# Column-quarter sums of a gated recurrent layer: squares, gates and dots in one group, and the sums of o's squares taken once in the feed-forward

## The chip, the cores and the metric

The kernel runs on one core of a Trainium2 chip. The metric is the device time of one execution in microseconds (us). Three runs of the kernel before took 1411.43, 1412.17 and 1412.77 us; the median is 1412.17. One more execution was profiled: 1412.02 us, of which the profile's span, from the first to the last instruction, is 1410.2.

The core has five engines that run side by side, each with its own queue of instructions: TensorE (PE in the profile, its weight loads PEld), VectorE (DVE), ScalarE (ACT), GpSimd (POOL) and SyncE (SP). Here SP only issues transfers (DMAs), and POOL issues those that add to what lies at their target.

## The reference

The input x is one sequence of 2048 tokens with 512 channels. After a layer norm (xn) two branches are computed and multiplied:

```
q, k, v = conv4(silu(xn @ W))          # 16 heads of 128, causal depthwise conv of 4 taps
q, k    = rope(q), rope(k), each divided by its norm over the head
out     = sum over lags s = 0..3 of (q . k[t-s]) * D**-0.5 * sigmoid(a[t-s] * b) * v[t-s]
s       = (out * rsqrt(mean(out**2) + eps) * norm_w * silu(xn @ Wz)) @ Wout
g       = silu((relu(xn @ sign(Wup).T * up_scale) @ sign(Wdown).T) * down_scale * out_scale)
result  = x + s * g
```

a and b are xn @ Wa and xn @ Wb, one number a head. Three kinds of sums over a head or over all channels matter here: the squares of q and k (for their norms), the products of q with the lagged k (the dots), and the squares of out over all 2048 channels (for the root mean square).

## The kernel before, in words

Tokens run along the free axis, 512 to a block (TB), in NTB = 4 blocks; channels lie on the 128 partitions. The 16 heads are worked on two at a time, NP = 8 pairs p = 0..7 in a block.

**The attention's steps.** step(p, b) (line 608) is software-pipelined: it computes q, k and the products of pair p for block b+1, and v, the weighted sum and the gated output of pair p for block b. It is called for b = -1 (block 0's q and k alone, beside the feed-forward of the first 512 tokens), for b = 0, 1 and 2, and the last block's v part has a loop of its own (line 829). InOrder (line 68) keeps the order of the program on TensorE (pe), VectorE (dve) and, where it is used, POOL (pool); line 76, which most rows of the profile name, is its call. The other instructions of ACT, SP and POOL are put in order by the planner that builds the program. In a step TensorE makes pq (16 passes), pk, pv, on even p the output projection po of two finished pairs (four chunks c of 8 passes), and pz.

**Column quarters.** The sums over partitions are matmuls with 32 columns of weights; add (line 429) sends the result to one of four strips of 32 partitions of a bank (tile_position). Four matmuls to the four strips run together. An f32 matmul stands in the trace as two passes, so a group of four appears as x8. The kinds are:
- squares: products (line 366) squares q and k into sq0 and sq1 (line 384), a POOL transfer adds the two, and sum_squares (line 434) adds a pair's sums. Two pairs fill the four strips. It is called in products on even p, between pk and pv, and at a change of block before norms.
- dots: sum_dots (line 445), four strips for the four lags. It is called in output_projections (line 596): halfway through po (after two chunks) when one is due, at once otherwise.
- gates: gate_products (line 231) makes a and b, ab in the profile; four stores to ab_dram follow, three of them accumulating, on POOL. It is called for block 0 after step 0, and for block b+2 in step 7 before pv. gate (line 251) reads them back later.
- sums of o (so): sums_of_o (line 454), two strips, once a block, after the block's last output projection. Its input is a tile squares[b] in pool vs: ACT writes the squares of pair 0's o there, and for the others ACT writes them to o2 (in xnT's first block, or for b = 0 in the second half of the weighted sum's tile te2) and a POOL transfer adds them to squares[b]. Two small transfers put the result in ss_dram.

**Pools.** vs holds what the v part needs (weights, v, bc, te, oz, z, wo, part). mm is a pool of six banks of PSUM. att.close() (line 873) gives back vs, mm and the rest, and the feed-forward opens the pools ff (SBUF, on the same side as vs), ph (three banks) and pf (four banks). ff's first transfers are the loads of down (3 x 1 MB, POOL) and of x, y and g (256 KB each, SP).

**The feed-forward.** For b = 1, 2, 3 and hidden chunks f, TensorE makes ph (8 passes in two f32r terms), ACT and VectorE turn it into hid, and two iterations later pf takes it (8 passes over four banks). Two chunks are made ahead, in the attention's last banks (line 866). ends (line 882) loads x, y and g for a block; gate scales y by rms, which comes from ss_dram by one load, a square root on ACT and a reciprocal on VectorE (lines 870 to 872), and multiplies the branches.

Of the kernel before, what the change touches and what calls it, by code (L numbers as in the profile page):

```python
# [54 lines left out]
TB = 512  # L55
# [26 lines left out]
def recurrent_layer(ctx: ExitStack, tc: tile.TileContext, a: dict, out: bass.AP):  # L82
# [29 lines left out]
    ab_dram = dram.tile([LW, HALO + S], F32, name="ab_dram")  # L112
    ss_dram = dram.tile([NTB, TB], F32, name="ss_dram")
    signs_dram = {n: dram.tile([P, NFC, HID], F32R, name=f"{n}_signs") for n in ("up", "down")}
    f_dram = dram.tile([TB, HID], F32, name="f_dram")
# [77 lines left out]

    means = {}
    means = {}
# [170 lines left out]
    def products(p, b, q, between=None, beside_k=None):  # L366
# [16 lines left out]

        sq = [qks.tile([P, 2, TB], F32, tag=f"sq{j}", name=f"sq{j}" + n, bufs=2 - j) for j in range(2)]
        for j in range(2):
# [48 lines left out]
    def sum_squares():  # L434

        if not squares_due:
            return
        if squares_due[0][0] == 0:
            banks["squares"] = sums.tile([P, TB], F32, tag="squares", name="squares")
        for p, sq in squares_due:  # L440
            for i in (1, 0):
                add(banks["squares"], 2 * (p % 2) + 1 - i, of_head[:, p], sq[:, i, :], p < 2, p >= NP - 2)
        squares_due.clear()

# [8 lines left out]

    def sums_of_o(b):

        so = mm.tile([P, TB], F32, tag="mm", name=f"so{b}")
        for j in range(2):
            add(so, j, ones, squares[b][:, j], True, True)
        row = vs.tile([P, HID], F32, tag="part", name=f"so_sb{b}", bufs=4)
        nc.scalar.copy(row[0 : 2 * LW], so[0 : 2 * LW])  # L460
        nc.gpsimd.dma_start(ss_dram[b : b + 1], row[0:1])
        nc.gpsimd.dma_start(ss_dram[b : b + 1], row[LW : LW + 1], accum_op=ALU.add)

    squares = {}
    rows = {}
# [59 lines left out]
    def weighted(p, b, v):  # L525
# [19 lines left out]
        dve.tensor_tensor(o, o, parts[0][:, 1], ALU.add)  # L545

        if p == 0:
            squares[b] = vs.tile([P, 2, TB], F32, tag="ss", name=f"ss{b}", bufs=1)
            nc.scalar.activation(squares[b], o, AF.Square)
        else:  # L550

            o2 = xnT[:, p % 2 * 2 : p % 2 * 2 + 2, HALO : HALO + TB] if b else parts[1][:, 0]
# [55 lines left out]
    def step(p, b, beside_q=None, beside_k=None):  # L608
# [6 lines left out]
        if change and b:  # L615
            sum_squares()
            norms(b)
# [19 lines left out]

        output_projections(sum_dots if due else None)
        if change:
# [65 lines left out]
    with tc.tile_pool(name="pre", bufs=1, side="right") as pre:  # L705
# [64 lines left out]
        for p in range(NP):  # L770
# [9 lines left out]
            if p + 2 < NP:  # L780
                fetch(*groups[p + 2])
            if p == 0:
                gate_products(0)
            elif p == 2:
                gate(0)
# [10 lines left out]
    load(vs, "z", 0, last)  # L796
    sum_squares()
    norms(last)
# [70 lines left out]
    nc.sync.dma_start(out_scale, a["out_scale"].partition_broadcast(P))  # L869
    nc.sync.dma_start(ss_acc, ss_dram.rearrange("b (c p) -> p (b c)", p=P))  # L870
    nc.scalar.activation(rms, ss_acc, AF.Sqrt, bias=eps_rms, scale=1.0 / CH)
    dve.reciprocal(rms, rms)
    att.close()

    with tc.tile_pool(name="ff", bufs=1, side="right") as ff, tc.tile_pool(
        name="ph", bufs=3, space=PSUM
    ) as phs, tc.tile_pool(name="pf", bufs=1, space=PSUM) as pfs:
        down = ff.tile([P, NFC - NFD, HID], F32R, name="down")
        for f in range(NFD, NFC, G):
            nc.gpsimd.dma_start(down[:, f - NFD : f - NFD + G], signs_dram["down"][:, f : f + G])  # L880

        def ends(b, banks=None):
# [54 lines left out]
        for b in range(1, NTB):  # L937
            pf = [pfs.tile([P, HID], F32, name=f"pf{c}") for c in range(TC)]
            for f in range(2, NFC + 2):
# [6 lines left out]
                if b == 1 and f == 2:  # L946
                    scale, gate = ends(0)
                if b == 1 and f in (6, 8, 10, 12):
                    scale(f // 2 - 3)
                    gate(f // 2 - 3)  # L950
                if b > 1 and f < 2 + TC:
# [111 lines left out]
```

## Time and profile before

| | us |
|---|---|
| time, median of three runs | 1412.17 |
| time of the profiled execution | 1412.02 |
| its span | 1410.2 |
| TensorE busy (3970 passes) | 1399.2 (99%) |
| VectorE busy | 1197.2 (85%) |
| ACT busy | 610.3 (43%) |
| POOL busy | 237.3 (17%) |
| squares: 128 passes of 128x32 weights | first 72.0, last 1046.1 |
| dots: 168 passes | first 53.4, last 1054.2 |
| gates (ab): 32 passes | first 31.2, last 738.9 |
| sums of o (so): 16 passes | first 503.8, last 1226.3 |

The page begins with a busy line for each engine. A line of the timeline has the start, the length, the engine, the source line, the operation, the tiles (out<-in), the shapes and the number of instructions merged into it; in brackets stand the idle time of the engine just before it and what ended it, so far as semaphores show it. Passes overlap, so the distance of two starts tells more than the lengths. A line of transfers has the tiles, the queue, the number, the size of each and the median time from issue to landing.

### The profile page before, as it was taken

To read this page: it belongs to the slowest core of one execution; us is meant where nothing else is said; L and a number is where in the kernel's file an instruction comes from. 1 tells how busy PE (TensorE), PEld (TensorE's weight loads), DVE (VectorE), ACT (ScalarE), POOL (GpSimd) and SP (SyncE) were. 2 spreads that over 40 slices of the span, in tenths; PEclk is the share of its full clock that TensorE was granted. 3 is DMA by queue.
4 is the path that set the end of the run, shared out by engine and by line. 5 is a ranking of instruction groups with operands and counts; after the bars stand their busy time and mean duration, and the time that the engine had idled before them with its cause. 6 is when DMAs were issued, how large, how long until landed. Compare 5 with 4: busy or idle time off the path is not lost.

```text
span 1410.2 us, 12492 instructions
## 1 busy us (share of the span) xinstructions
PE 1399.2 (99%) x3970; PEld 687.7 (49%) x3970; DVE 1197.2 (85%) x1243; ACT 610.3 (43%) x1181; POOL 237.3 (17%) x317
## 2 busy tenths in 40 slices
PE   9999999999999999999999999999999999999998
PEld 6555544344444444444444444444444444578886
DVE  7999999999999999999999899999994998146454
ACT  7566555445444544454434534444442333232122
POOL 2222121111212121112122212121211121200000
PEclk9999999999999999999999999999999999999999
DMA  9989577988988689978985799787848998672020
GB/s 316 284 226 198 126 200 170 238 217 173 199 215 194 141 181 237 227 175 191 224 187 143 163 233 216 178 193 177 165 93 199 226 257 186 123 246 89 24 90 30
DMA packets 104465, 259.21 MB, mean 184 GB/s; under 512 B 18832, under 2 KB 19344, under 8 KB 100048
## 3 DMA queue, kind: packets, MB, share of 16 engines
q0 software_dynamic: 35776, 104.89, 38.3%
q1 hardware_dynamic: 68624, 153.53, 37.5%
q8 instruction: 32, 0.52, 0.1%
q14 instruction: 33, 0.27, 0.1%
HBM read 157.67 MB, written 35.68 MB: 137 GB/s over the span
## 4 chain that ended last, share of the span: by engine, by line
PE 58%; DVE 28%; DMA 5%; issue 4%; ACT 3%; SPq 1%; POOL 0%; DVEq 0%; ACTq 0%; POOLq 0%
PE pq L76 9%; DVE q L76 8%; PE pk L76 8%; PE ph L76 8%; PE pf L76 8%; PE pz L76 8%; PE po L76 8%; DVE te L76 7%; PE pv L76 6%; DVE v L76 4%; DVE k L76 4%; DVE pr L76 3%; DMA bc<-co_dram 2%; DMA co_dram<-rk 1%; PE dots L76 1%
## 5 line engine op out<-in xcount | busy, mean ns | idle before, releaser
L76 PE MATMUL po<-wo,oz 128*128 128x512 f32 x512 | 225.9, 595 | 1.6 <-DVE oz L76 1.6
L76 PE MATMUL pq<-xnT,wq 128*128 128x512 f32 (+1 forms) x528 | 226.5, 581 | 0.2 <-ACT xnT L76 0.2
L76 PE MATMUL pv<-xnT,wv 128*128 128x512 f32 x512 | 226.4, 594 | 0.0
L76 PE MATMUL pz<-xnT,wz 128*128 128x512 f32 x512 | 225.3, 592 | 0.5 <-ACT rv L313 0.5
L76 PE MATMUL pk<-xnT,wk 128*128 128x512 f32 x512 | 225.2, 592 | 0.0
L76 DVE SCALAR_TENSOR_TENSOR k<-rk,conv_w,k 128x512 f32<-128x512 f32 x192 | 142.1, 751 | 24.1 <-ACT k L325 19.5
L76 DVE TENSOR_TENSOR te<-v,bc 128x2048 f32<-128x2048 f32 x64 | 143.9, 2288 | 19.4 <-DMA bc<-co_dram 18.1
L76 PEld LDWEIGHTS pq<-xnT,wq 128*128 128x128 f32 x528 | 98.7, 189 | 124.5 <-issue 113.4
L76 PEld LDWEIGHTS po<-wo,oz 128*128 128x128 f32 x512 | 96.1, 190 | 128.6 <-issue 110.0
L76 PEld LDWEIGHTS pv<-xnT,wv 128*128 128x128 f32 x512 | 95.7, 189 | 127.7 <-issue 116.9
L76 DVE SCALAR_TENSOR_TENSOR q<-rq,conv_w,q 128x512 f32<-128x512 f32 x192 | 141.5, 749 | 19.3 <-ACT q L325 14.8
L76 PEld LDWEIGHTS pz<-xnT,wz 128*128 128x128 f32 x512 | 96.5, 189 | 124.6 <-issue 118.7
L76 PEld LDWEIGHTS pk<-xnT,wk 128*128 128x128 f32 x512 | 96.6, 189 | 120.5 <-issue 116.9
L76 DVE SCALAR_TENSOR_TENSOR v<-rv,conv_w,v 128x512 f32<-128x512 f32 x192 | 141.3, 750 | 6.9 <-ACT v L325 2.4
L76 DVE SCALAR_TENSOR_TENSOR q<-q,turns 128x1024 f32<-128x1024 f32 (+1 forms) x128 | 127.1, 1014 | 2.3
L76 DVE TENSOR_TENSOR pr<-q,k 128x2048 f32<-128x2048 f32 x52 | 117.3, 2286 | 0.9
L700 ACT ACTIVATE hid<-ph,up_scale 128x512 f32<-128x512 f32 x64 | 44.0, 687 | 120.5 <-PE ph L76 118.5
L76 DVE CAST hid_hi<-hid 128x512 fp32r<-128x512 f32 x64 | 27.2, 425 | 71.8 <-ACT hid L700 71.8
L76 PE MATMUL ph<-xs_hi,up 128*128 128x512 f32 x192 | 76.4, 398 | 0.7 <-ACT so_sb L460 0.7
L76 PE MATMUL ph<-xs_lo,up 128*128 128x512 f32 x192 | 75.8, 395 | 0.0
L76 DVE TENSOR_TENSOR te<-te,te 128x2048 f32<-128x2048 f32 x32 | 73.3, 2292 | 1.1
L594 POOL DMA_DIRECT2D s_dram<-part x48 | 50.7, 1231 | 70.1 <-ACT part L588 66.5
(147 smaller groups left out, 1655.4 us busy)
## 6 DMA issues: line engine op xcount, KB each, us to landing
bc<-co_dram SPq DMA_DIRECT2D x128, 256.0 KB, 7.3
pr<-pr POOLq DMA_DIRECT2D x72, 256.0 KB, 6.4
wq<-in_wq_dram SPq DMA_DIRECT2D x32, 512.0 KB, 6.6
wk<-in_wk_dram SPq DMA_DIRECT2D x32, 512.0 KB, 6.6
sq<-sq POOLq DMA_DIRECT2D x32, 512.0 KB, 6.5
wv<-in_wv_dram SPq DMA_DIRECT2D x32, 512.0 KB, 8.0
wz<-in_wz_dram SPq DMA_DIRECT2D x32, 512.0 KB, 5.7
wo<-in_wo_dram SPq DMA_DIRECT2D x32, 512.0 KB, 6.3
```

The source lines that it names most:

```text
L76: return self.tc.keep_in_program_order(getattr(self.engine, op)(*args, **kwargs))
L594: nc.gpsimd.dma_start(rows, part, accum_op=ALU.add)
L700: nc.scalar.activation(hid, ph, AF.Relu, scale=up_scale[:, f : f + 1])
```

## The change

The sums of squares and the gates move to where the dots are. A function strips in step runs halfway through the output projection on even p (or wherever dots are due): the squares of the pairs p-2 and p-1, on p = 6 the gates of block b+2 (on p = 1 of b = -1 those of block 0), and the dots that are due. sum_squares takes the pair at which it stops. sq0 has three buffers instead of two. gate(0) comes after step 3 instead of step 2.

The squares of o are no longer summed in SBUF. All pairs write o2, and POOL's transfers go to o2_dram, pair 0's plainly and the others accumulating. The four blocks' squares are loaded (512 KB each, SP) as the first tile of ff, ss; sums_of_o runs once, in the first feed-forward block at f = 4, between ph and pf, with four strips for the four blocks, and its copy goes to ss_dram by four small transfers on SP. The root and the reciprocal come at f = 8 instead of at the end of the attention, and the first block's scale and gate at f = 8, 10, 12, 14 instead of 6, 8, 10, 12.

```diff
+    o2_dram = [dram.tile([P, 2, TB], F32, name=f"o2_dram{b}") for b in range(NTB)]
...
-        if p % 2 == 0:
-            sum_squares()
+        if p == 0:
+            sum_squares(p)
...
-        sq = [... bufs=2 - j) for j in range(2)]
+        sq = [... bufs=3 - 2 * j) for j in range(2)]
...
+    def sum_squares(last):
+        while squares_due and squares_due[0][0] != last:
+            p, sq = squares_due.pop(0)
+            if p == 0:
+                banks["squares"] = sums.tile([P, TB], F32, tag="squares", name="squares")
             for i in (1, 0):
                 add(banks["squares"], 2 * (p % 2) + 1 - i, of_head[:, p], sq[:, i, :], p < 2, p >= NP - 2)
...
+        o2 = xnT[:, p % 2 * 2 : p % 2 * 2 + 2, HALO : HALO + TB] if b else parts[1][:, 0]
+        nc.scalar.activation(o2, o, AF.Square)
         if p == 0:
-            squares[b] = vs.tile([P, 2, TB], F32, tag="ss", name=f"ss{b}", bufs=1)
-            nc.scalar.activation(squares[b], o, AF.Square)
+            pool.dma_start(o2_dram[b], o2)
         else:
-            o2 = xnT[...] if b else parts[1][:, 0]
-            nc.scalar.activation(o2, o, AF.Square)
-            pool.dma_start(squares[b], o2, accum_op=ALU.add)
+            pool.dma_start(o2_dram[b], o2, accum_op=ALU.add)
...
-        if p == NP - 1:
-            outputs_due.append(lambda midway: sums_of_o(b))
...
-        if p == NP - 1 and b + 2 < NTB:
-            gate_products(b + 2)
...
-        output_projections(sum_dots if due else None)
+        def strips():
+            if p and p % 2 == 0:
+                sum_squares(p)
+            if p == NP - 2 and b + 2 < NTB:
+                gate_products(b + 2)
+            if p == 1 and not at:
+                gate_products(0)
+            if due:
+                sum_dots()
+        output_projections(strips if p % 2 == 0 or due else None)
...
-    nc.sync.dma_start(ss_acc, ss_dram.rearrange("b (c p) -> p (b c)", p=P))
-    nc.scalar.activation(rms, ss_acc, AF.Sqrt, bias=eps_rms, scale=1.0 / CH)
-    dve.reciprocal(rms, rms)
     att.close()
...
+        ss = ff.tile([P, NTB, 2, TB], F32, name="ss")
+        for b in range(NTB):
+            nc.sync.dma_start(ss[:, b], o2_dram[b])
         down = ff.tile([P, NFC - NFD, HID], F32R, name="down")
...
+        def sums_of_o():
+            so = phs.tile([P, TB], F32, name="ph")
+            for j in range(2):
+                for b in range(NTB):
+                    add(so, b, ones, ss[:, b, j], j == 0, j == 1)
+            row = ff.tile([P, TB], F32, name="row")
+            nc.scalar.copy(row, so)
+            for b in range(NTB):
+                nc.sync.dma_start(ss_dram[b : b + 1], row[LW * b : LW * b + 1])
+            nc.sync.dma_start(ss_acc, ss_dram.rearrange("b (c p) -> p (b c)", p=P))
...
+                if b == 1 and f == 4:
+                    sums_of_o()
+                if b == 1 and f == 8:
+                    roots()
+                if b == 1 and f in (8, 10, 12, 14):
+                    scale(f // 2 - 4)
+                    gate(f // 2 - 4)
```

More of the change, by code (lines that the diff above doesn't have):

```diff
@@ L192, in first_layer_norm @@
         return lambda: (transpose(2), transpose(3))
-    means = {}
     means = {}
@@ L382, in products @@
             beside_k()
-        sq = [qks.tile([P, 2, TB], F32, tag=f"sq{j}", name=f"sq{j}" + n, bufs=2 - j) for j in range(2)]
+        sq = [qks.tile([P, 2, TB], F32, tag=f"sq{j}", name=f"sq{j}" + n, bufs=3 - 2 * j) for j in range(2)]
         for j in range(2):
@@ L432, in add @@
         pe.matmul(rows, heads, src, start=start, stop=stop, tile_position=(0, LW * s))
[L434 to L440, printed above, removed]
+    def sum_squares(last):
[3 more added lines that the diff above has]
+                banks["squares"] = sums.tile([P, TB], F32, tag="squares", name="squares")
             for i in (1, 0):
                 add(banks["squares"], 2 * (p % 2) + 1 - i, of_head[:, p], sq[:, i, :], p < 2, p >= NP - 2)
-        squares_due.clear()
     def sum_dots():
@@ L452, in sum_dots @@
                 add(banks["dots"], s, heads, pr[:, s, :], p == 0, last and pr is prs[-1])
[L454 to L464, printed above, removed]
     rows = {}
@@ L545, in weighted @@
         dve.tensor_tensor(o, o, parts[0][:, 1], ALU.add)
+        o2 = xnT[:, p % 2 * 2 : p % 2 * 2 + 2, HALO : HALO + TB] if b else parts[1][:, 0]
+        nc.scalar.activation(o2, o, AF.Square)
         if p == 0:
-            squares[b] = vs.tile([P, 2, TB], F32, tag="ss", name=f"ss{b}", bufs=1)
-            nc.scalar.activation(squares[b], o, AF.Square)
-        else:
-            o2 = xnT[:, p % 2 * 2 : p % 2 * 2 + 2, HALO : HALO + TB] if b else parts[1][:, 0]
-            nc.scalar.activation(o2, o, AF.Square)
-            pool.dma_start(squares[b], o2, accum_op=ALU.add)
+            pool.dma_start(o2_dram[b], o2)
+        else:
+            pool.dma_start(o2_dram[b], o2, accum_op=ALU.add)
         return o
@@ L615, in step @@
         if change and b:
-            sum_squares()
+            sum_squares(p)
             norms(b)
@@ L636, in step @@
             v = values(p, b, raw)
-        output_projections(sum_dots if due else None)
+        def strips():
+            if p and p % 2 == 0:
+                sum_squares(p)
+            if p == NP - 2 and b + 2 < NTB:
[5 more added lines that the diff above has]
+        output_projections(strips if p % 2 == 0 or due else None)
         if change:
@@ L781, in recurrent_layer @@
                 fetch(*groups[p + 2])
-            if p == 0:
-                gate_products(0)
-            elif p == 2:
+            if p == 3:
                 gate(0)
@@ L796, in recurrent_layer @@
     load(vs, "z", 0, last)
-    sum_squares()
+    sum_squares(None)
     norms(last)
@@ L880, in recurrent_layer, with roots @@
             nc.gpsimd.dma_start(down[:, f - NFD : f - NFD + G], signs_dram["down"][:, f : f + G])
+        def sums_of_o():
[8 more added lines that the diff above has]
+            nc.sync.dma_start(ss_acc, ss_dram.rearrange("b (c p) -> p (b c)", p=P))
+        def roots():
+            nc.scalar.activation(rms, ss_acc, AF.Sqrt, bias=eps_rms, scale=1.0 / CH)
+            dve.reciprocal(rms, rms)
         def ends(b, banks=None):
@@ L947, in recurrent_layer @@
                     scale, gate = ends(0)
-                if b == 1 and f in (6, 8, 10, 12):
-                    scale(f // 2 - 3)
-                    gate(f // 2 - 3)
+                if b == 1 and f == 4:
[5 more added lines that the diff above has]
+                    gate(f // 2 - 4)
                 if b > 1 and f < 2 + TC:
```

## The prediction

> **What bounds the kernel now.** I read the page's busy line first, then TensorE's timeline at the places the change touches, then the queues at the start of the feed-forward.
>
> Busy line of the page, and TensorE's timeline at 0, 207 to 355 and 1098 us:
>
> ```profile
> PE 1399.2 (99%) x3970; PEld 687.7 (49%) x3970; DVE 1197.2 (85%) x1243; ACT 610.3 (43%) x1181; POOL 237.3 (17%) x317
> ...
> 1.59 4.63 PE L76 MATMUL unread<-still 128*128 128x512 f32 x6 [1.59 <-DVE still L665]
> ...
> 207.42 7.14 PE L76 MATMUL pv<-xnT,wv 128*128 128x512 f32 x16
> 214.49 1.92 PE L76 MATMUL dots<-pr,of_head 128*32 128x512 f32 x16
> 216.34 7.14 PE L76 MATMUL pq<-xnT,wq 128*128 128x512 f32 x16
> 223.31 7.03 PE L76 MATMUL pk<-xnT,wk 128*128 128x512 f32 x16
> ...
> 264.62 1.07 PE L76 MATMUL squares<-sq,of_head 128*32 128x512 f32 x8
> ...
> 272.59 1.88 PE L76 MATMUL po<-wo,oz 128*128 128x512 f32 x4
> 276.02 5.42 PE L76 MATMUL po<-wo,oz 128*128 128x512 f32 x12 [1.55 <-DVE oz L76]
> ...
> 330.54 7.03 PE L76 MATMUL pk<-xnT,wk 128*128 128x512 f32 x16
> 337.51 1.06 PE L76 MATMUL squares<-sq,of_head 128*32 128x512 f32 x8
> 338.50 7.14 PE L76 MATMUL pv<-xnT,wv 128*128 128x512 f32 x16
> 345.47 7.03 PE L76 MATMUL po<-wo,oz 128*128 128x512 f32 x16
> ...
> 1098.30 7.14 PE L76 MATMUL pz<-xnT,wz 128*128 128x512 f32 x16 [0.54 <-ACT rv L313]
> ```
>
> TensorE sets the time: 99% busy, and a run of 16 full passes takes 6.87 us wherever it stands, 0.43 a pass. It waits in three places only: 1.7 us at 274 (for oz), 0.7 at 1097, 0.7 at 1227 (below). Elsewhere a us off TensorE is a us off the kernel, as long as nothing is late.
>
> TensorE, POOL and SP where the feed-forward begins, then transfers issued at 1227 and at 1234 to 1236, and the engines' table for 1237 to 1246 and for the end (its last columns are granted clock, DMA share and GB/s):
>
> ```profile
> 1226.31 1.05 PE L76 MATMUL so<-ss,ones 128*32 128x512 f32 x4
> 1228.08 0.51 PE L76 MATMUL ph<-xs_hi,up 128*128 128x512 f32 x1 [0.72 <-ACT so_sb L460]
> ...
> 1231.53 0.76 POOL L462 DMA_DIRECT2D ss_dram<-so_sb  x1 [2.67 <-DMA ss_dram<-so_sb]
> 1234.50 1.69 POOL L880 DMA_DIRECT2D down<-down_signs  x3 [2.21 <-PE ph L76]
> ...
> 1234.60 0.71 SPq L889 DMA_DIRECT2D x<-in_x_dram  x1
> ...
> s_dram<-part POOLq DMA_DIRECT2D x1, 256.0 KB, 3.7
> ...
> down<-down_signs POOLq DMA_DIRECT2D x3, 1024.0 KB, 8.4
> x<-in_x_dram SPq DMA_DIRECT2D x1, 256.0 KB, 6.9
> y<-s_dram SPq DMA_DIRECT2D x1, 256.0 KB, 9.3
> ...
> 1237.00:1246.00 9.00, 8.77 (x37) 6.70 (x37) 4.32 (x9) 1.55 (x3) 0.00 (x0) 1.00 1.06 404
> 1407.30:1410.20 2.90, 0.00 (x0) 0.00 (x0) 0.00 (x0) 0.00 (x0) 0.00 (x0) 0.50 0.24 90
> ```
>
> The point is the hour at which pool ff opens. Its first loads, down on POOL and x on SP, go to different tiles from different queues, and both leave at 1234.5 to 1234.6. The last transfer out of the old pool vs, so_sb's second (issued 1231.53, 2.1 to land), landed at 1233.6. So ff opens as a whole, 0.9 us after vs's last transfer; PE, which the line names, had been done with vs since 1228.
>
> **Switches saved.** A lone group of strips: pk to pv 7.96 us instead of 6.87, and pv to po 6.97 instead of 6.87, so 1.19. Two groups in one (dots x16): pv at 207.42 to pk at 223.31 is 15.89 against 13.74 for two runs; 0.10 of it belongs to the group before pv, so 2.05. A merge saves 2x1.19-2.05 = 0.33; eight passes more cost 0.86. Twelve groups of squares (steps 2, 4, 6 of four blocks) join dots, and three of gates (block 0 beside dots at step 1; blocks 2 and 3 beside squares and dots at step 6) lose a group of their own: 15x0.33 = 5.0 us. The group of block 1 already lay beside dots.
>
> **Sums of o out of the attention.** Three lone groups of four passes go at 1.18 each (503.8, 790.5, 1069.0): 3.5. At the end ph waited until 1228.08 for so_sb's copy; now the last thing in the old banks is the copy of po, 1226.46 to 1227.05: ph starts 1.0 earlier, and 0.1 goes with the switch. The one group in the feed-forward has 16 passes: 2.05 added. Net 3.5+1.1-2.05 = 2.6.
>
> **What of this does not arrive.** At 274 TensorE waits for oz, and VectorE runs without a gap from 218 to 345, so it sets the hour there. The squares at 264.62 lay ahead of this wait, where they were free; behind it they cost 0.86 and the merge's 0.33 saves nothing: 1.2 lost. At 1097 pz waits for ACT's rv, behind a VectorE that waited 12.0 us for bc; the group removed at 1069 only lengthens this wait: 1.2 lost. So 7.6-2.4 = 5.2 us are gained, the new group paid.
>
> In the other blocks oz ends 1.2 to 5.0 us before po starts (least at 345 and 847, 1.2 and 1.5); po now comes 1.19 earlier in each such step, as the squares ahead of it go. It just fits. VectorE waits for TensorE's k and q in each later step (0.7 to 1.8 us), so it can follow.
>
> **Edits at nothing.** The third buffer of sq0 holds squares that are now read half a step later; the sums they wait for landed long before. Divide at step 5 ends 8 us before the gates' new slot (VectorE 158.3 and 413.3, slots 168 and 423). o2's transfers go on POOL as before, 512 KB each, to DRAM; s_dram's accumulations run beside them now. Four are new, at step 0, 0.9 to 1.2 us of POOL each, and POOL is 17% busy; behind the new wait for Square lie the next pr and sq, 14 us ahead of need. In block 0, step 0's transfer reads te2, which VectorE writes again at 269.3; Square ends at 262.1, so 7.2 us remain. The same tile's 512 KB took 5.0 to 12.5 (median 8.9) accumulating; without reading the target I take it as landed. Bounds 0 and 1.7 (median), on the path at 274 if it comes. The gates' four stores, one after the other (ten waits of POOL for them take 47.3 us), go on POOL in step 6 instead of 7, ahead of two part stores and o2's transfer: some 14 us, where part has four buffers and po comes again 45 us later. The rms chain (copy 0.6, stores 2.5, load 2.9, root with table 1.9) stands behind x, y and g in SP's queue (3.1 MB, 8 us): 16 us against the 15 from the sums to f = 8, and the next hid has two iterations (7.5 us) to spare.
>
> **What it adds on the path: the load of ss.** The four ss tiles (2.1 MB) can't leave before ff opens. The last transfer out of vs is now the part issued at 1227.34, landed 3.7 later at 1231.1; opening takes 0.9, so 1232.0. A load shows nothing for 1.9 us (wo, 512 KB issued at 1200.4, landed in 3.2, of which 1.3 is its bytes at 400 GB/s). At the same moment POOL starts down, 3.1 MB. Together 5.24 MB at 404 GB/s take 13.0 us. While down runs, SP's queue gets the small share: x and y, 256 KB each, landed 3.2 us apart, 82 GB/s of the 404. So ss ends last, at 1232.0+1.9+13.0 = 1246.9. TensorE stands before sums_of_o when ph of f = 4 is done: before that was 1237.5, now 1236.5. It works in order, and down's pf, the next ph and every later product are queued behind. The wait is 10.4 us. If ss had the engines alone, 2.1 MB in 5.2 us, it would be 2.6; those are the ends, and I take the upper, as the row of x and y is the same queue against the same down.
>
> Ten idle us also cost clock. The last pass ends at 1404.1, and at 1407.2 the granted clock falls to 0.50 (last line above), so a wait of 10.4 us ends in a slow array. What it takes to wake it is seen at the start only: six unread passes took 4.63 us, 0.85 from start to start, twice the 0.43: five starts late by 2.1. I take 2.0; the range has nothing (rival 2) and 3, half as much again.
>
> The Trainium skill speaks against this step (TensorE: Matmul & The Clock Gate, Why this matters for your kernels): it wants no idle gap over about 3 us between bursts of matmuls, since one idle window returns the array to half clock, and its Part 1 gives some 3.4 us of work before full clock is back. By that page alone the slow stretch would lose some 1.7 us, an estimate, and the time would be 1419.1; the trace agrees on the gap (3.1 us), and no run here shows the return in mid-kernel yet.
>
> Sum: -5.2+10.4+2.0 = +7.2 on the profiled run's 1412.02 (span 1410.2 and 1.8 around it); its median is 0.15 higher: **1419.4 us**.
>
> **Rivals.** (1) ss first. If SP's queue is served ahead of down, the wait is 2.6, no slow clock: -2.6, 1409.6, faster. For it: SP's issue has less to do than POOL's three (1.69 us). Against: the row of x and y. It turns at a wait of 5.2, ss landed by 1241.7. (2) The wait in full, the clock unharmed: 1417.4. Against: the fall to 0.50 after 3.1 us. (3) VectorE sets the blocks' time, as oz is down to 0.3 us ahead at 847 and te2's cover may fail: of the 5.2 none to half arrives, 1422 to 1424.6. Against: its waits for k and q. (4) ss lands between 1240 and 1244 as down starts late: 1411 to 1415.
>
> **How the numbers follow.** Forecast 0.56, rival 2 0.08, rival 3 0.15, rival 1 0.12, rival 4 0.09. Range: 1411 leaves out most of rival 1, 1422.5 the worse half of rival 3. No change means within 0.2% (2.8 us, what a measurement can tell): slower are the forecast and rivals 2 and 3, 0.79; faster rival 1 with a little of 4, 0.12; same 0.09. The forecast's own range is 1417 to 1421.
>
> **What would show it.** Right: squares and dots x16, at step 6 x24, one switch each; ff's first loads at about 1226 (5 to 6 earlier than 1232); a wait of so for ss of 8 us or more at f = 4, and passes 0.85 apart behind it. Wrong: so without a wait, down landing after ss, or waits of po for oz in each block.

## The result and the profile after

The changed kernel took 1420.02 us (median of 6 runs, 1419.02 to 1422.53) against 1412.20 for the kernel before on the same chip; the ratio is 1.0057 with a 95% interval of 1.0044 to 1.0070. The forecast was 1419.4. The profiled execution took 1419.02 us, its span is 1417.2: 7.0 more than before.

The total is right, but partly by luck: each of the four terms that it is added up from is off by 1.5 to 2.1 us as far as the medians tell, two to each side, and they cancel. The busy line of the page first: TensorE's busy time has fallen by 2.0 us while the span grew by 7.0.

```profile
PE 1397.2 (99%) x3970; PEld 691.0 (49%) x3970; DVE 1197.1 (84%) x1243; ACT 604.7 (43%) x1177; POOL 233.0 (16%) x313
```

TensorE's timeline of the changed kernel, at 257 to 290, at 1094 and at 1232 to 1245 (columns as in the prediction):

```profile
267.80 8.80 PE L76 MATMUL pv<-xnT,wv 128*128 128x512 f32 x16 [4.08 <-DMA wv<-in_wv_dram]
276.44 7.03 PE L76 MATMUL po<-wo,oz 128*128 128x512 f32 x16
283.40 1.07 PE L76 MATMUL squares<-sq,of_head 128*32 128x512 f32 x8
284.28 1.04 PE L76 MATMUL dots<-pr,of_heads 128*32 128x512 f32 x8
...
1094.37 7.14 PE L76 MATMUL pz<-xnT,wz 128*128 128x512 f32 x16 [0.35 <-ACT rv L313]
...
1232.70 1.15 PE L76 MATMUL ph<-ss,ones 128*32 128x512 f32 x4
1237.92 1.92 PE L76 MATMUL ph<-ss,ones 128*32 128x512 f32 x2 [4.07 <-DMA ss<-o_dram]
1241.69 3.30 PE L76 MATMUL ph<-ss,ones 128*32 128x512 f32 x10 [1.86 <-DMA ss<-o_dram]
...
1244.92 0.50 PE L76 MATMUL pf<-first_down,hid_hi 128*128 128x512 f32 x1
```

The reader sees the change at work (squares and dots back to back, one switch), and two waits that were not there. The sums of o's squares occupy TensorE from 1232.70 to 1244.92, 12.2 us. At 263 pv waits 4.1 us for its weights, where before the squares stood and nothing waited; pv itself then takes 8.80 instead of 7.14. The same pv in TensorE's timeline of the kernel before:

```profile
265.61 7.14 PE L76 MATMUL pv<-xnT,wv 128*128 128x512 f32 x16
```

The timeline of the changed kernel on VectorE at the same place, and on SP and POOL at the opening of ff:

```profile
266.44 2.29 DVE L76 TENSOR_TENSOR te<-v,bc 128x2048 f32<-128x2048 f32 x1
270.12 2.29 DVE L76 TENSOR_TENSOR te<-v,bc 128x2048 f32<-128x2048 f32 x1 [1.39 <-DMA o_dram<-te]
...
1228.28 1.76 SPq L870 DMA_DIRECT2D ss<-o_dram  x4
1228.77 1.65 POOL L873 DMA_DIRECT2D down<-down_signs  x3 [3.79 <-DMA s_dram<-part]
```

The engines' table of the changed kernel for parts of 1238 to 1248 (busy time of PE, PEld, DVE, ACT and POOL; the last three columns are granted clock, DMA share and GB/s):

```profile
1238.00:1240.00 2.00, 1.83 (x2) 0.10 (x2) 0.00 (x0) 0.00 (x0) 0.00 (x0) 0.50 1.06 420
1242.00:1244.00 2.00, 2.00 (x9) 0.36 (x2) 0.00 (x0) 0.00 (x0) 0.00 (x0) 0.50 1.04 398
1246.00:1248.00 2.00, 2.00 (x10) 1.63 (x9) 0.00 (x0) 0.00 (x0) 0.00 (x0) 1.00 1.05 391
```

VectorE waits 1.39 us before it may write te2 again, since pair 0's squares are still being read out of it (issued 261.81, landed 8.3 us later). ss and down leave within half a microsecond of each other; ss's last tile landed at 1241.69, 13.4 us after the first of the four was issued, with the transfers at 400 GB/s throughout; down's last tile landed later still, at 1243.76. While TensorE waited, the granted clock fell to 0.50.

To see where time goes, I set the start of each pass against that of the same pass in the profiled execution of before. A negative number is earlier. The first column is an offset that arises in the first 20 us of an execution, whatever the kernel; it is to be taken off the others. The last two columns are VectorE's. The runs are told below.

| run | TensorE at 20 | 285 | 505 | 998 | 1070 | 1098 | 1160 | VectorE at 300 | 1020 |
|---|---|---|---|---|---|---|---|---|---|
| the changed kernel | -0.43 | +2.89 | +0.70 | -2.82 | -3.63 | -3.93 | -3.92 | +0.88 | -0.02 |
| e4_own_later | -0.21 | +1.87 | -0.32 | -3.84 | -4.92 | -4.96 | -4.95 | -0.34 | -1.61 |
| e6_squares_ahead | -0.06 | +1.33 | -0.85 | -3.52 | -3.64 | -3.91 | -3.91 | +1.33 | -0.05 |
| e9_mended | -0.08 | +3.56 | +1.38 | -2.15 | -3.22 | -3.06 | -3.30 | -0.25 | -0.50 |
| e10_mended_all | -0.35 | -0.50 | -2.69 | -4.67 | -4.75 | -5.26 | -5.26 | -0.30 | -1.17 |
| e11_o_only | -0.66 | -0.69 | -1.87 | -3.05 | -4.12 | -3.33 | -3.32 | -0.68 | -0.68 |
| e12_lighter | -0.46 | -2.79 | -4.97 | -8.50 | -9.57 | -10.38 | -10.94 | -2.88 | -8.89 |

In the changed kernel ph of the feed-forward started 4.91 earlier than before (1223.17 against 1228.08): 0.4 of it is the offset, 3.5 come from the blocks and 1.0 from the release of the old banks. The forecast had 7.2 there. The group of the sums then cost 11.9, where the forecast had 14.4.

### The profile page after: what moved, and what is told of

Its sections match the earlier page's. It is cut to its first block, busy times and chain, and to the rows that moved or that the text cites. A ratio compares the mean times of both kernels' runs of the same rounds, so it can differ in the third digit from the quotient of the medians.

```text
span 1417.2 us, 12490 instructions
## 1 busy us (share of the span) xinstructions
PE 1397.2 (99%) x3970; PEld 691.0 (49%) x3970; DVE 1197.1 (84%) x1243; ACT 604.7 (43%) x1177; POOL 233.0 (16%) x313
## 5 line engine op out<-in xcount | busy, mean ns | idle before, releaser
L76 DVE SCALAR_TENSOR_TENSOR k<-rk,conv_w,k 128x512 f32<-128x512 f32 x192 | 142.0, 751 | 24.1 <-ACT k L325 19.6
L388 POOL DMA_DIRECT2D sq<-sq x32 | 34.1, 1066 | 173.2 <-ACT sq L387 86.3
```

What stands on the lines that cost most here:

```text
L76: return self.tc.keep_in_program_order(getattr(self.engine, op)(*args, **kwargs))
L388: nc.gpsimd.dma_start(sq[0], sq[1], accum_op=ALU.add)
```

## The experiments

The kernel before took 1411.9 to 1412.1 us (medians) beside them. Edits are against the changed kernel unless another is named.

**The sums four iterations later: is the wait the load's?**

```diff
-                if b == 1 and f == 4:
+                if b == 1 and f == 8:
                     sums_of_o()
-                if b == 1 and f == 8:
+                if b == 1 and f == 12:
                     roots()
...
+                if b == 1 and f in (12, 13, 14, 15):
+                    scale(f - 12)
+                    gate(f - 12)
```

> The sums of o's squares four iterations later (f = 8 instead of 4), the root at f = 12, block 0's ends at f = 12 to 15. Theory (TensorE waits for ss because pool ff opens late and down shares the engines): four iterations are 15 us, more than the 9 us by which ss was late, so the group costs its 2.05 us alone, no wait, no slow passes behind it: 9 to 10 us below the changed kernel, 1410 to 1411.5. Rival (the cost lies in the group or in the chain of the root behind it): within 2 us of 1420.

Measured: 1412.71 us (10 runs), 1.0008 of before (0.9998 to 1.0017). The sums waited for nothing and cost 1.85 us instead of 12.2, a gain of 10.4. But four of them came back: at the start of the next block pf waited for VectorE's scale, which stood behind four ends and the 3.5 us of xs, all between f = 12 and 15. The eight passes of f32r tiles behind this wait then stood 0.43 apart instead of 0.23, at a granted clock of 0.50. TensorE's timeline of this run, and the engines' table:

```profile
1288.86 0.40 PE L76 MATMUL ph<-xs_lo,up 128*128 128x512 f32 x1
1291.27 0.64 PE L76 MATMUL pf<-first_down,hid_hi 128*128 128x512 f32 x1 [2.00 <-DVE g L76]
...
1292.00:1293.00 1.00, 1.00 (x4) 0.78 (x4) 1.00 (x2) 0.97 (x2) 0.00 (x0) 0.50 0.00 0
```

So the wait at f = 4 is the load's, and the place of the ends is a second thing to get right.

**Down behind ss: do the two loads share the transfers' rate?** A transfer of 16 bytes out of ss makes POOL wait until ss has landed before it issues down; down's loads go through pool too, which keeps the order.

```diff
+        mark = dram.tile([1, 4], F32, name="mark")
+        pool.dma_start(mark, ss[0:1, NTB - 1, 1, 0:4])
         down = ff.tile([P, NFC - NFD, HID], F32R, name="down")
```

> down's loads may start only when the last ss tile has landed (a 16-byte transfer out of ss stands ahead of them on POOL). Theory (the two queues share the engines, ss has the smaller part): ss then has the engines nearly alone, 2.1 MB at 400 GB/s, and lands about 7.5 us after its issue instead of 13.4; the wait at the sums falls from 9 to about 3 us and the time by about 6, unless down, now late by as much, is waited for at f = 6 (then 0 to 4 of the 6 come back there). Rival (ss takes its 13 us whatever runs beside it): the wait stays at 9, and the time is the changed kernel's or more.

Measured: 1412.24 us (10 runs), 1.0005 of before (0.9995 to 1.0014), and 6.0 us less than the changed kernel at this place (7.8 between the medians; the rest is not explained). ss, issued from 1228.64 on, landed at 1237.1, 8.5 us after the first issue instead of 13.4, and TensorE's timeline has one wait of 1.59 and one of 0.21, after which the ten passes take 1.90 instead of 3.30:

```profile
1235.86 1.05 PE L76 MATMUL ph<-ss,ones 128*32 128x512 f32 x2 [1.59 <-DMA ss<-o_dram]
1237.11 1.90 PE L76 MATMUL ph<-ss,ones 128*32 128x512 f32 x10 [0.21 <-DMA ss<-o_dram]
1238.95 0.50 PE L76 MATMUL pf<-first_down,hid_hi 128*128 128x512 f32 x1
```

The Trainium skill (DMA: Bandwidth & Descriptors, Queues, rings and completion order) says that each transfer engine goes round the queues that have work, a packet at a time; this case agrees, as ss ahead of down is done 4.9 us sooner than beside it.

**Pair 0's squares in a tile of their own: what does te2 cost?** In the first block pair 0's squares go to a spare oz buffer; in the second kernel their transfer also leaves one step later, so that it is out of the way of pv's weights.

```diff
+        if p == b == 0:
+            o2 = vs.tile([P, 2, TB], F32, tag="oz", name="first_o2", bufs=3)
         nc.scalar.activation(o2, o, AF.Square)
```

> Pair 0 of block 0 writes its squares to a buffer of oz that is free then, not into te2; the transfer to DRAM goes as before. Theory (te2's second writer waits for that transfer): VectorE's wait of 1.39 us for it at 270 is gone; pv's wait for wv at 263 (4.2 us) stays, as the transfer still runs beside wv. po at 276 is then bound by wv, so the time falls by 0 to 0.5. Rival (wv's wait comes from te2's wait): both go, 2.5 us less.

> As the run before, and the transfer of pair 0's squares is issued only after pair 1's, some 14 us later. Theory (that transfer takes the engines from wv): wv lands by 265.5 as in the kernel before, pv waits 1 to 2 us at most (it comes 1.1 us earlier than before), po waits for oz about as before; 2.5 to 3 us less than the changed kernel. Rival (wv is late for another reason, such as the order on SP's queue): pv's wait of 4 us stays.

Measured: 1417.97 us (one run) and 1417.90 us (median of 4; 1.0041 of before, 1.0026 to 1.0056). VectorE's wait of 1.39 is gone, and the gain of 2.1 us is the same with and without the delay. My theory that this transfer also holds up wv fell: pv still waited 3.5 and 2.9 us.

**What makes wv late?** SP's timeline has it. Before, x_in of step 1 left at 253.2, ahead of two bc loads; in the changed kernel the planner put it at 256.2, between them and wv. A row of SP's timeline of the kernel before, then two of the changed kernel:

```profile
253.22 0.35 SPq L204 DMA_DIRECT2D x_in<-in_x_dram  x1
...
256.18 0.60 SPq L204 DMA_DIRECT2D x_in<-in_x_dram  x1
256.88 0.38 SPq L268 DMA_DIRECT2D wv<-in_wv_dram  x1
```

Here it is moved ahead of all bc loads.

```diff
+        if p == 1 and b == 0:
+            statistics(2, 1)
         if p == 1 and at:
             gate(b + 1)
...
-            if p < TC:
+            if p < TC and (p, b) != (1, 0):
                 statistics(b + 2, p)
```

> The changed kernel with one load moved: in the first block, x_in of step 1 is issued on SP ahead of the first bc loads (and of the gate's rows), no longer directly ahead of wv. Theory (the wait of pv at 263 comes from the place that the planner gave x_in's load: before, it left at 253.2, ahead of the two bc loads; after, at 256.2, between them and wv, so 256 KB more stood ahead of wv at 200 GB/s, 1.3 us): wv lands 1 to 2 us sooner after its issue (8 to 9 us instead of 9.4 to 10.8), pv's wait falls from 2.9 to 4.2 us to 1.5 to 2.5, and TensorE stands 1 to 2 us earlier at 285 than in the changed kernel; 1418 to 1419 us. Rival (the traffic of the whole stretch makes wv late, in whatever order it is issued): wv lands 9.4 or more after its issue, the wait stays at 3 us or more, time 1419 to 1420.5. If the first products of VectorE wait for bc because x_in goes ahead of it, 1 us is lost at 240 and this shows in the idle time of VectorE there.

Measured: 1419.21 us (4 runs, 1417.61 to 1420.92), 1.0054 of before (1.0036 to 1.0072). wv landed 8.2 us after issue (10.8 in the changed kernel, 7.8 before) and pv waited 1.6, as the theory had it (the row names ACT's k; wv landed at 264.93, 0.14 before pv began). But TensorE was not earlier at 285: po now waits for oz, that is for VectorE, which had lost its time at te2. TensorE's timeline of this run:

```profile
265.07 7.11 PE L76 MATMUL pv<-xnT,wv 128*128 128x512 f32 x16 [1.60 <-ACT k L325]
272.01 1.88 PE L76 MATMUL po<-wo,oz 128*128 128x512 f32 x4
276.51 7.11 PE L76 MATMUL po<-wo,oz 128*128 128x512 f32 x12 [2.62 <-DVE oz L76]
```

**The first block's squares back ahead of pv.**

```diff
-        if p == 0:
+        if p == 0 or (p, b) == (2, 1):
             sum_squares(p)
```

> The changed kernel with the squares of the first block's step 2 back ahead of pv; all other groups as changed. Theory (they cost nothing there, as pv waits for wv anyway; behind pv they cost 0.86 and the saved switch of 0.33 is worth nothing): pv starts when wv lands, as in the changed kernel, and the group of strips at 283 is 0.9 to 1.2 us shorter, so TensorE stands 0.9 to 1.2 us earlier at 285 and at every later place up to the feed-forward; its idle time at 263 falls by the 1.0 us that the squares take, so that fewer of the passes behind it are at half clock, another 0 to 1 us. 1418 to 1419.2 us. Rival (VectorE sets the hour at 276 and hands the gain back): 1419.5 to 1420.5, with a wait of po for oz of 1 us.

Measured: 1419.12 us (4 runs), 1.0049 of before (1.0033 to 1.0065). TensorE was 1.6 us earlier than in the changed kernel at 285, somewhat more than expected, kept 0.7 of it to 998, and had none left behind the dots at 1052. These waited for pr, a product of VectorE whose halves a transfer adds. The timeline of this run, a row of TensorE and one of VectorE:

```profile
1051.54 1.07 PE L76 MATMUL dots<-pr,of_heads 128*32 128x512 f32 x8 [0.88 <-DMA pr<-pr]
...
1020.79 2.33 DVE L76 SCALAR_TENSOR_TENSOR q<-rq,conv_w,q 128x512 f32<-128x512 f32 x3 [1.31 <-ACT q L325]
```

The same row of VectorE in the timeline of the kernel before:

```profile
1020.84 2.32 DVE L76 SCALAR_TENSOR_TENSOR q<-rq,conv_w,q 128x512 f32<-128x512 f32 x3 [1.31 <-ACT q L325]
```

VectorE does the same at the same time, although TensorE was 3.5 us ahead of before at 998 and at 1040. Its waits of 1.3 and 1.8 us here are for ACT's first product of the convolution (L325), and they keep their length however early TensorE is: those for k add up to 19.5 us before, 19.6 in the changed kernel and 19.4 in e10_mended_all. What ACT's product stands behind is seen in the timelines of ACT and VectorE of e11_o_only (told below), in which TensorE is 2.4 us ahead at this place:

```profile
1022.52 1.15 ACT L354 ACTIVATE q<-q,turns 128x1024 f32<-128x1024 f32 x1 [1.91 <-DVE q L76]
1023.58 0.71 ACT L325 ACTIVATE k<-rk,conv_w 128x512 f32<-128x512 f32 x1
...
1024.32 4.57 DVE L76 SCALAR_TENSOR_TENSOR k<-rk,conv_w,k 128x512 f32<-128x512 f32 x6 [1.83 <-ACT k L325]
```

ACT waited for VectorE's q, and VectorE then for ACT: the chain goes from VectorE over ACT back to VectorE, without TensorE. That is a second chain as long as TensorE's.

**Down behind ss, and the sums one iteration later.** Against e2_down_behind.

```diff
-                if b == 1 and f == 4:
+                if b == 1 and f == 5:
                     sums_of_o()
```

> As the run in which down's loads leave only when ss has landed, and the sums of o's squares one iteration later, at f = 5, where TensorE comes 6.9 us later. Theory (ss lands at about 1237, TensorE comes to the sums at about 1239.6, so nothing waits; the group costs its 16 passes and one switch, 2.05, instead of 12.2, and no clock is lost; the roots at f = 8 stand as late as they did, since the chain of rms waits for down's bytes on the wire until 1252): TensorE at the start of f = 8 is 9.5 to 10.2 us earlier than in the changed kernel, total 1409 to 1410.5 us. Rival (the chain of rms is now late for f = 8, ACT stands before the root and the next hid with it): a wait of pf for hid of 1 to 4 us after f = 8, 1411 to 1414.

Measured: 1414.44 us (median of 10 runs, 1412.90 to 1418.87 but for one of 8400.3 us, which nothing here explains), 1.0021 of before (1.0009 to 1.0032): worse than expected by 4 to 5 us. The sums waited for nothing, but the loads only changed places: TensorE now comes sooner to the first product with down, and down, held back behind ss, was late. Behind this wait the passes of f32r tiles stood 0.43 apart instead of 0.23, and the granted clock was 0.50 for 3.41 us. TensorE's timeline and the engines' table:

```profile
1244.87 0.47 PE L76 MATMUL pf<-down,hid_hi 128*128 128x512 f32 x1 [2.68 <-DMA down<-down_signs]
...
1246.00:1247.00 1.00, 1.00 (x4) 0.81 (x3) 0.00 (x0) 0.00 (x0) 0.00 (x0) 0.50 1.13 440
```

The profiled execution took 1412.9, the lowest of this kernel's runs; what the others lost beyond that stays open.

**Passes that keep TensorE busy during the wait.** This was to measure the clock.

```diff
+            for _ in range(15):
+                pe.matmul(so, up_of(0)[:, 0], xs[0][:, 0], start=True, stop=True)
```

> The changed kernel with 15 extra passes of an up block (their result is overwritten) ahead of the sums of o's squares, in the time in which TensorE waits for ss: 6.5 us of work from 1232.7 to 1239.2; ss still lands at 1241.7. Theory (a wait ends in passes at half clock, and these cost 1.5 to 2 us): the passes behind the wait are 0.43 apart instead of 0.85, the granted clock stays at 1.00, and from 1250 on everything is 1.3 to 2.0 us earlier than in the changed kernel: 1418 to 1418.8 us. Rival (the passes 0.85 apart come from the data or the loads, not from the idle time): they stay 0.85 apart and the time is 1419.5 to 1421.

Measured: 1418.37 us (4 runs), 1.0043 of before (1.0027 to 1.0059). It settles nothing: I had taken 0.43 us for a pass, but passes of f32r tiles stand 0.23 apart, so the filler lasted 3.6 us, waits of 0.3 and 2.7 followed it, and the clock fell again, for 3.41 us instead of 6.83. Of the 1.5 us that TensorE was earlier behind the sums, 1.05 were there ahead of them. The engines' table of this run:

```profile
1238.00:1240.00 2.00, 0.00 (x0) 0.00 (x0) 0.00 (x0) 0.00 (x0) 0.00 (x0) 0.91 1.05 409
1240.00:1242.00 2.00, 1.72 (x9) 0.39 (x10) 0.00 (x0) 0.00 (x0) 0.00 (x0) 0.50 1.03 396
```

**The mended kernel**: pair 0's squares as in e4_own_later, the loads as changed, the sums at f = 7, the ends on both sides of f = 12.

```diff
-                if b == 1 and f == 4:
+                if b == 1 and f == 7:
                     sums_of_o()
-                if b == 1 and f == 8:
+                if b == 1 and f == 10:
                     roots()
-                if b == 1 and f in (8, 10, 12, 14):
-                    scale(f // 2 - 4)
-                    gate(f // 2 - 4)
+                if b == 1 and f in (10, 11, 13, 14):
+                    c = (10, 11, 13, 14).index(f)
+                    scale(c)
+                    gate(c)
```

> The changed kernel with two repairs: in the first block pair 0's squares of o go to a spare oz buffer and leave one step later, and the sums of o's squares come three iterations later (f = 7), the roots at f = 10, the ends of the first block's rows at f = 10, 11, 13 and 14; ss and down are loaded as in the changed kernel. Theory: ss has landed (1241.7) when TensorE comes to the sums at about 1243, so the group costs 2 us instead of 12.2 and no pass is at half clock (10 us less); VectorE does not wait for te2 (1.2 to 2.1 us less, as measured by that edit alone); nothing of it comes back, since the ends are spread around the work of f = 12: 1407.3 to 1409.0 us, faster than the kernel before by 0.2 to 0.35%. Rival (the ends make VectorE late for the next block's pf, as they did when they all stood at f = 12 to 15, or the chain of rms is late for f = 10): a wait of pf or of hid of 1 to 4 us after 1250, 1410 to 1413.

Measured: 1407.49 us (5 runs, 1405.67 to 1409.23), 0.9965 of before (0.9953 to 0.9977). It beats both kernels: 4.6 us less than before, 12.5 less than the change as made. The group of sums is one run of 16 passes, 1.85 us from start to the next start, and nothing waits behind it. TensorE's timeline:

```profile
1244.54 1.92 PE L76 MATMUL ph<-ss,ones 128*32 128x512 f32 x16
1246.39 0.50 PE L76 MATMUL pf<-down,hid_hi 128*128 128x512 f32 x1
```

**The mended kernel with both edits of the first block** (x_in first, squares ahead).

> As the mended kernel, and in the first block the squares of step 2 stand ahead of pv and x_in of step 1 is loaded ahead of bc. Theory (from 1000 on VectorE sets the hour: with one of these edits alone TensorE was 0.7 to 1.6 us earlier than in the changed kernel up to 982, and at 1052 it waited for pr and had 0 to 0.1 of it left): the wait of pv for wv falls to 1 us or less, TensorE stands 1 to 3 us earlier than in the mended kernel between 290 and 980, dots waits for pr at 1050 for as much, and the time is that of the mended kernel within 0.8 us. Rival (TensorE sets the hour, the waits found were of the run): 2 to 3 us less than the mended kernel, 1404.5 to 1406.5.

Measured: 1407.21 us (6 runs), 0.9966 of before (0.9953 to 0.9979): no different from the mended kernel. (The profiled execution of the mended kernel was the slowest of its runs, 1409.2 us, and the one here an ordinary one, so the table's last columns show more between them than the medians do.) TensorE was 4 us earlier than in the mended kernel up to 500 and 2.5 at 998, and has new waits for oz, wk and pr in its timeline (the view of wk's row ends at 830, so it counts three passes of 16):

```profile
275.52 1.98 PE L76 MATMUL po<-wo,oz 128*128 128x512 f32 x4 [1.25 <-DVE oz L76]
828.80 1.53 PE L76 MATMUL pk<-xnT,wk 128*128 128x512 f32 x3 [1.08 <-DMA wk<-in_wk_dram]
1050.44 1.06 PE L76 MATMUL dots<-pr,of_heads 128*32 128x512 f32 x8 [0.93 <-DMA pr<-pr]
```

**The mended kernel without the merges**: squares and gates in groups of their own at their old places, sq0 with two buffers.

```diff
-        if p == 0:
-            sum_squares(p)
+        if p % 2 == 0:
+            sum_squares(None)
...
-        output_projections(strips if p % 2 == 0 or due else None)
+        output_projections(sum_dots if due else None)
```

> The mended kernel without the merges: squares and gates stand in groups of their own where the kernel before had them; only the sums of o's squares are changed, with both repairs. By the terms of the prediction: three groups of 1.18 and 1.1 at the end saved, 2.05 added, 2.6 us less than the kernel before, 1409.4 us; the merges are then worth what lies between this run and the mended one. Theory (VectorE sets the hour at 1050, so that what TensorE saves in the blocks arrives in part): 1 to 2 us between the two. Rival (TensorE alone counts, so the merges bring 15 switches less the one at 274, 3.8 us): 3 to 4 us.

Measured: 1409.24 us (10 runs, 1407.12 to 1410.01), 0.9976 of before (0.9968 to 0.9985). The sums of o alone, well placed, bring 2.9 us; the merges the 1.75 between this run and the mended one, though the two intervals touch. VectorE kept the hour of before throughout the three blocks (-0.68 at 269 and at 1020, the offset of this execution), while TensorE came 3.5 ahead; at 1095 it waited for rv, in TensorE's timeline:

```profile
1094.97 7.14 PE L76 MATMUL pz<-xnT,wz 128*128 128x512 f32 x16 [1.44 <-ACT rv L313]
```

**VectorE relieved.** Against the mended kernel with both edits; the first three blocks' outputs lack half of their lags.

```diff
-        dve.tensor_tensor(o, o, parts[0][:, 1], ALU.add)
+        if b == last_block:
+            dve.tensor_tensor(o, o, parts[0][:, 1], ALU.add)
```

> The last kernel with both edits in the first block (squares ahead, x_in first), and VectorE relieved: in the first three blocks weighted leaves out its last addition, the sum of the two halves of te (1.23 us a step, 24 steps), so that the outputs of these blocks lack half of their lags; TensorE's work is the same. Theory (from 270 to 1100 VectorE's chain sets the hour wherever TensorE has got ahead of it): the waits of TensorE for oz at 274 (1.3), for pr at 1049 (0.9) and for rv at 1092 (0.3) are gone, VectorE's products of the last block start 2 us earlier or more than without this edit, TensorE stands at 1095 2 to 3 us earlier, and the time is 1403.5 to 1405.5 us. Rival (transfers or TensorE itself set the hour, VectorE only follows): 1406.5 to 1408 us, with the waits for pr and rv as they are.

Measured: 1401.82 us (5 runs, 1401.49 to 1402.61), 0.9931 of before (0.9917 to 0.9944). TensorE's work is the same, and the time is 5.4 us less, more than I expected: the four waits for oz, wk, pr and rv are all gone, and from 998 to 1160 TensorE is 3.8 to 5.7 us earlier. At 1088 in TensorE's timeline pz waits for nothing:

```profile
1087.92 7.03 PE L76 MATMUL pz<-xnT,wz 128*128 128x512 f32 x16
```

So VectorE's chain (with ACT's products in it), and not TensorE alone, sets the time of the attention.

## Why the prediction was right, and where it was not

The total held: forecast 1419.4, measured 1420.0; slower by 0.6% as the likeliest case had it. That the main cost is the wait for ss was foreseen; that the sum came out within 1 us was luck. Point by point, with the runs that measured each term (differences of medians, each with about 2 us of doubt by the intervals; for the last two terms the traces above bear them out):

| term | forecast | measured | by |
|---|---|---|---|
| sums of o out of the blocks, new group paid | -1.4 (-2.6, of which 1.2 lost) | -2.9 | e11_o_only against before |
| merges | -3.8 (-5.0, of which 1.2 lost) | -1.8 | e9_mended against e11_o_only |
| te2 read by a transfer | 0 (bounds 0 and 1.7) | +2.1 | the changed kernel against e4_own_later |
| wait for ss and the slow clock | +12.4 (+10.4 and +2.0) | +10.4 | e4_own_later against e9_mended |
| sum | +7.2 | +7.8 | |

**The price of a switch** was right: from one merge of squares and dots to the next TensorE's starts are 0.33 to 0.34 us earlier (+2.89 at 285 and +2.55 at 356, +0.37 at 569 and +0.04 at 640, -2.15 at 855, -2.49 at 926 and -2.82 at 998), and 1.18 where a group of so is gone. What failed is not the price but how much of it arrives.

**The load of ss** was right in place and cause: it can't leave before ff opens, and down takes a share of the rate, as e2_down_behind shows. Rival 1 (ss first) is out. Mis-sized was that share, and with it "ss ends last": the prediction gave SP's queue 82 of the 404 GB/s while down runs, and ss got some 183 (an estimate: 2.1 MB from 1230.2, 1.9 us after the first issue, to 1241.69). So down landed after ss, by 2.1 us, which the prediction had named as a sign of being wrong. Two of the tiles had landed when TensorE came at 1232.70, the third came 5.2 us later and the fourth 9.0, while the transfers ran on at 385 GB/s until 1250. The wait ended 9.0 us after TensorE had come, and not 10.4, and six of the group's 16 passes ran before its end. Rival 4's window, 1240 to 1244, holds the landing at 1241.69 only because TensorE and with it the opening of ff came about 4 us earlier than in the hours in which the prediction counts; down did not start late (0.5 us after ss), and the time lies outside its 1411 to 1415.

**The clock** was in place and a little smaller: the ten passes behind the wait took 3.23 us to the next start, and 1.84 in e2_down_behind, where the granted clock stayed at 1.00; that is 1.4 against 2.0. The Trainium skill (TensorE: Matmul & The Clock Gate, Why this matters for your kernels) names a gap of about 3 us; the gap here was longer and the clock fell, but in other runs shorter waits were enough (2.68 us in e7_sums_at_5, 2.00 in e1_sums_late), and there the measurement decides. Rival 2 is out. That filling the wait would save it was not shown, since my filler was too short.

**"In block 0, step 0's transfer reads te2 ... I take it as landed"** failed. The transfer took 8.3 us where 7.2 remained, near the median of the row that I had used for the upper bound; the lower end was the wrong choice. Its price of 2.1 is above my bound of 1.7, since VectorE's lost time stays lost: with the offsets taken off, VectorE is 1.4 us later at 300 than with the tile repaired, and 0.8 to 1.8 at 1020.

**"It just fits. VectorE waits for TensorE's k and q in each later step, so it can follow"** failed, and is the main error. The rows name ACT's q and k (L325), not TensorE's, and ACT stood behind VectorE; in e11_o_only and e6_squares_ahead VectorE's hour is the same at 1020 as before (0.02 and 0.01 off, the offsets taken off) with TensorE 2.4 and 3.5 us ahead. Single gains of TensorE in the blocks of 1.6 and 4 us (e6, e10) were worth 0.9 and 0.3 us in the median, within the spread of the runs. In the changed kernel itself the limit hardly shows: TensorE stood 3.3 us late at 285, and the merges behind that place arrived in full up to 998. Rival 3 had the mechanism, and "none to half arrives" is what the merges show, 1.8 of 5.0; I gave it 0.15 because I read the wait's releaser wrongly. Its figure is out all the same: of the 5.2 us in all, 4.6 arrived in the mended kernel, since the sums of o brought more than forecast.

**"1.2 lost at 1097"** was wrong for this kernel: the group removed at 1069 arrived (-3.63 at 1070, -3.93 at 1098), and pz's wait for rv went from 0.54 to 0.35. In e11_o_only it was lost in part (-4.12, then -3.33).

**"1.2 lost at 274"** was right in kind and too small in size. The squares there had covered the landing of wv; without them and with x_in ahead of it, pv waited 4.1 us and some of its passes ran at half clock, and TensorE stood 3.3 us later than before at 285, the offset taken off. Little of that is in the end time, as e6_squares_ahead and e10_mended_all show, because VectorE would have taken it back later. The sum also counted 1.3 us for the four merges that lie ahead of this wait, though VectorE sets the hour behind it: in e10_mended_all TensorE was 0.5 us earlier than before at 240, and after this wait 0.2, as much as VectorE.

Of the edits at nothing, the third buffer of sq0, the gates' stores, gate(0)'s later place and the rms chain let TensorE wait nowhere. At 131, ahead of all this, the starts of pf go from -1.25 to -0.60: pf waits for VectorE's hid_lo, which comes at the hour of before (130.71 against 131.18, less the offset of 0.43). There too a gain of TensorE ends at VectorE.

## What to carry to other kernels

When one engine is 99% busy and another 85%, trace the second one's chain before you count a gain on the first: if its starts do not move when the first gets ahead, it is a bound too, and its waits are not slack. A load that can leave only when a pool opens shares the rate with all that leaves with it; put its reader later by all these bytes over the rate, and move what depends on it to both sides of the next heavy piece. A tile that is also the source of a transfer is free only when the transfer has landed; take the row's median, not the hope.

## What the runs showed of the hardware that I had not expected

The clock can give way after a shorter wait than the 3.1 us that the prediction went by, and the length of the wait alone does not decide it. Between the first and the last pass the stretches at a granted clock of 0.50 last 3.41, 6.83 or 10.24 us in every trace, and within one execution their starts lie whole multiples of 3.413 us apart (268.32 and 1237.71 in the changed kernel, 284 of them; 267.47 and 1291.47 in e1_sums_late, 300). Where this grid lies differs from one execution to the next: full clock, which also begins on it, was first granted 4.6 to 7.8 us after the start.

With each execution cut into steps of 3.413 us on its own grid, one rule fits all 14 traces. A step at full clock in which TensorE was idle for 1.83 us or more was followed by half clock each time, 17 times between 30 and 1400 us (least 1.83 in e6_squares_ahead at 264 and 2.00 in e1_sums_late at 1289); a step with 1.76 or less never was (most in e7_sums_at_5 at 263). So the wait of 2.00 in e1_sums_late, which fell into one step, cost the clock, and waits of 2.12 and 2.30 in e7_sums_at_5 (at 263 and 275), which fell across two, did not. A slow stretch of 3.41 us near 270 cost 1.6 to 1.8 us in eight executions, and one of 6.83 cost 3.0 (e9_mended at 267).
